# dt of a selective scan from ScalarE's softplus table, and silu of z where z is made

## Chip, cores and metric

The kernel runs on one core of a Trainium2 chip. The metric is the device time of one execution, in microseconds. All runs told here were in the fast state. "Before" is the tuned kernel, "after" the changed one. Engine names are those of the profile: PE (TensorE, products), DVE (VectorE), ACT (ScalarE), POOL (GpSimd). The granted clock is the share of the full TensorE clock that the profile shows, averaged over a stretch (PEclk).

## The reference, cut to what matters

Four images of 48 x 48 positions go through a layer with a two-dimensional selective scan, then attention, then a long spectral convolution.

```python
dts = einsum('bkrl,kdr->bkdl', dts_r, dt_proj_w)
dt  = softplus(dts + dt_proj_b)                      # what the change is about
...
def step(h, inp):                                    # scan over 2304 positions, 4 directions
    dA = exp(dt_l[..., None] * A)
    h  = h * dA + (dt_l * u_l)[..., None] * B_l
    y  = einsum('bkdn,bkn->bkd', h, C_l)
...
y = layernorm(y) * silu(z)                           # the change's second part
```

## The kernel before: the parts concerned

An image is scanned in 24 chunks of 384 positions (4 directions x 6), a chunk in 8 units (2 channel halves x 4 groups of states), a unit in 4 scans. Every engine works its instructions in the order of the program. Under the scans of images 1 to 3, PE runs the long convolution of the image before, fed in between so that it ends with the scans.

dt is prepared in pieces that are strewn over the units of the two chunks before. Softplus is built from relu, abs, exp and ln, all in one table set, and PE adds its four terms in PSUM:

```python
nc.scalar.activation(re[:, h, 1], ps[:, :CS], AF.Abs)       # per half, from PSUM
nc.scalar.activation(re[:, h, 0], ps[:, :CS], AF.Relu)
...
nc.scalar.activation(e, e, AF.Exp, scale=-1.0)              # both halves, 768 columns
nc.scalar.activation(u, e, AF.Identity, bias=1.0)
nc.scalar.activation(l, u, AF.Ln)
nc.scalar.activation(u, u, AF.Identity, bias=mone)
...
for h in range(NH):
    ps = mm_tile(...)                                       # one PSUM buffer of its own
    for i, (w, t) in enumerate(((ident, e[:, h]), (nident, u[:, h]), (ident, l[:, h]), (ident, re[:, h, 0]))):
        nc.tensor.matmul(ps[:, :CS], w, t, start=(i == 0), stop=(i == 3))
    nc.scalar.copy(re[:, h, 0], ps[:, :CS])                 # dt
    nc.vector.tensor_tensor(re[:, h, 1], ps[:, :CS], x, ALU.mult)   # dt * x, one operand in PSUM
```

The unit, which decides how waits spread:

```python
dA = exp(A * dt)                  # ACT, into one of two PSUM buffers, 4 per unit
tensor_tensor_scan(s, dA, s)      # DVE, 4 per unit
s = s * C                         # POOL, one product of 3.45 us per unit
y += csum^T s                     # PE
s_next = dt*x * B                 # DVE from PSUM (5 units of 8) or POOL (3 of 8)
```

Of the kernel before, what the change touches and what calls it, by code (L numbers as in the profile page):

```python
# [8 lines left out]
F32 = mybir.dt.float32  # L9
AF = mybir.ActivationFunctionType  # L10
ALU = mybir.AluOpType
# [4 lines left out]
P = 128  # L16
# [3 lines left out]
D, NS, R, K = 256, 16, 8, 4  # L20
NH = D // P
CS = 384
SUB = 384
# [31 lines left out]
def hybrid_kernel(ctx: ExitStack, tc: tile.TileContext, a: dict, out: bass.AP):  # L55
# [3 lines left out]
    nc = tc.nc  # L59
    ctx.enter_context(tc.manual_schedule())  # L60
    wp = ctx.enter_context(tc.tile_pool(name="w", bufs=1, side="left"))
# [5 lines left out]
    ident = wp.tile([P, P], F32, name="ident")  # L67
# [4 lines left out]
    def load(name, shape, src):  # L72
        t = wp.tile(shape, F32, name=name)
        nc.scalar.dma_start(t, src)
        return t

    win = load("win", [P, 2 * D], a["in_proj_wT"])
# [10 lines left out]
    owb = wp.tile([P, NH, C], F32, name="owb")  # L88
    nc.vector.tensor_scalar_mul(cw, cw, 0.5)
    nc.vector.tensor_scalar_mul(cb, cb, 0.5)  # L90
    for h in range(NH):
        nc.vector.tensor_scalar_mul(owb[:, h], owg[:, h], nb[:, h:h + 1])
        nc.vector.tensor_scalar_mul(owg[:, h], owg[:, h], ng[:, h:h + 1])
# [18 lines left out]
    nident = wp.tile([P, P], F32, name="nident")  # L112
# [11 lines left out]

    csum = wp.tile([P, DL], F32, name="csum")
    nc.vector.tensor_reduce(csum, ident.rearrange("p (c j) -> p j c", j=DL), AX.X, ALU.add)
    mone = wp.tile([P, 1], F32, name="mone")
    nc.vector.memset(mone, -1.0)
    shift = wp.tile([P, 1], F32, name="shift")
    nc.vector.memset(shift, -SHIFT)  # L130
    carry = wp.tile([P, NH, Q4, G4], F32, name="carry")
# [9 lines left out]
    def tokens(x, J):  # L141

        n = PIECES[J]
        return x[512 * J:512 * J + P * n].rearrange("(p j) c -> p j c", j=n)

    def exp_ln():

        nc.scalar.preload_act_table_set("natural_log_exp_and_others")

    def normed(x, d, eps, small, sq, name):  # L150

# [17 lines left out]
    def prologue(b, pool, mm_tile):  # L169
# [11 lines left out]
        xc = xcs[b] = [keep.tile([P, H, W], F32, tag=f"xc{h}", name=f"xc{b}_{h}") for h in range(NH)]  # L181
        rows, parts = SUB // W, SUB // P

        def cols(i):
            return slice(i * SUB, (i + 1) * SUB)
# [52 lines left out]
        def proj(h, i, z):  # L238
            now = {}

            def pe():
                now["ps"] = mm_tile(f"ip{b}_{h}_{i}_{z}")
                nc.tensor.matmul(now["ps"][:, :SUB], win[:, z * D + h * P:z * D + (h + 1) * P], xT[:, cols(i)],
                                 start=True, stop=True)

            def rest():
                if z:
                    t = pool.tile([P, SUB], F32, tag=f"z{i % 2}", name=f"z{b}_{h}_{i}")
                    nc.scalar.copy(t, now["ps"][:, :SUB])
                    nc.sync.dma_start(zs[h, :, cols(i)], t)  # L250
                    return
                nc.scalar.copy(xpad[:, 1 + i * rows:1 + (i + 1) * rows, 1:W + 1],
                               now["ps"][:, :SUB].rearrange("p (r w) -> p r w", w=W))
            tasks.append((pe, rest, not (h or i or z)))
# [27 lines left out]
        n = L // SUB  # L282
# [34 lines left out]
    def in_order(t, k, lo, n):  # L317

        if k % 2 == 0:
            return t[:, lo // W:(lo + n) // W, :]  # L320
        return t.rearrange("p h w -> p w h")[:, lo // H:(lo + n) // H, :]

    def mm_tile(name):
        return psm.tile([P, 512], F32, tag="mm", name=name)

    class Chunk:
# [16 lines left out]
        def prep(self, pool):  # L343




            k, name, xc = self.k, self.name, xcs[self.b]
            yield
            xd = self.xd = pool.xd.tile([64, CS], F32, tag="xd", name=f"xd{name}")  # L350
            bcd = self.bcd = dram.tile([32, CS], F32, tag="bcd", name=f"bcd{name}")
            ps = mm_tile(f"xp{name}")
            for h in range(NH):
                nc.tensor.matmul(ps[:64, :CS], xw[:, h, k, :], in_order(xc[h], k, self.lo, CS),
                                 start=(h == 0), stop=(h == NH - 1))
            yield 2 * CS
            nc.scalar.activation(xd, ps[:64, :CS], AF.Identity, bias=onerow)
            yield

            u, l = [pool.one.tile([P, NH, CS], F32, tag=f"tmp{v}", name=f"{v}{name}") for v in "ul"]  # L360
            re = pool.one.tile([P, NH, 2, CS], F32, tag="re", name=f"re{name}")
            for h in range(NH):
                ps = mm_tile(f"dt{name}_{h}")
                nc.tensor.matmul(ps[:, :CS], dtw[:, k, h * P:(h + 1) * P], xd[:R + 1], start=True, stop=True)
                yield CS
                nc.scalar.activation(re[:, h, 1], ps[:, :CS], AF.Abs)
                nc.scalar.activation(re[:, h, 0], ps[:, :CS], AF.Relu)
                if h == 0:
                    nc.sync.dma_start(bcd, xd[32:64])
                yield  # L370
            e = re[:, :, 1]
            yield 0
            nc.scalar.activation(e, e, AF.Exp, scale=-1.0)
            nc.scalar.activation(u, e, AF.Identity, bias=1.0)
            yield
            yield 0
            nc.scalar.activation(l, u, AF.Ln)
            nc.scalar.activation(u, u, AF.Identity, bias=mone)
            d = dram.tile([NH, DL, 2, G4, CS], F32, tag="dtdu", name=f"dtdud{name}")

            def store(h):
                for g in range(G4):
                    nc.sync.dma_start(d[h, :, :, g], re[g * DL:(g + 1) * DL, h])

            def load(h):
                rep = pool.rep.tile([P, 2, G4, CS], F32, tag="rep", name=f"rep{name}_{h}")
                for c in range(C4):
                    nc.sync.dma_start(rep[c * DL:(c + 1) * DL], d[h])
                self.rep.append(rep)

            yield
            for h in range(NH):
                ps = mm_tile(f"sp{name}_{h}")
                for i, (w, t) in enumerate(((ident, e[:, h]), (nident, u[:, h]), (ident, l[:, h]), (ident, re[:, h, 0]))):
                    nc.tensor.matmul(ps[:, :CS], w, t, start=(i == 0), stop=(i == 3))
                yield 4 * CS

                nc.scalar.copy(re[:, h, 0], ps[:, :CS])
                x = in_order(xc[h], k, self.lo, CS)
                w = x.shape[2]  # L400
                nc.vector.tensor_tensor(re[:, h, 1].rearrange("p (r w) -> p r w", w=w),
                                        ps[:, :CS].rearrange("p (r w) -> p r w", w=w), x, ALU.mult)
                if h == 1:
                    store(0)
                yield
            yield 0
            store(1)
            load(0)
            yield
            yield 0  # L410
            load(1)
            yield
# [60 lines left out]
    POOLED = ((0, 3), (1, 1), (1, 3))  # L473
    order = [(k, c) for k in range(K) for c in (range(NCH) if k < 2 else reversed(range(NCH)))]
    quads = [(h, q) for h in range(NH) for q in range(Q4)]
# [1 line left out]
    EARLY = 4  # L477
    FETCHED = sorted({q for h, q in POOLED} | set(range(Q4, 2 * Q4)))

    CHUNK_COLS = (len(quads) - len(POOLED)) * CS + len(quads) * CS + 12 * CS  # L480

    def begin_scans(b, pool):

# [12 lines left out]
    def scans(b, chunks, preps, front, sp, back, work, work_cols):  # L496

        units = [Unit(ch, h, q) for ch in chunks for h, q in quads]
        total = len(chunks) * CHUNK_COLS + work_cols
        done = [0]  # L500
# [75 lines left out]
    def epilogue(b, T, xn, xnT, tmp, pool, ps):  # L576
# [7 lines left out]
        zr, mu, o, sq, rd, lns, pt = {}, {}, {}, {}, {}, {}, {}  # L584
        var = ps.one.tile([P, 512], F32, tag="var", name=f"var{b}")

        def at(J):
            return slice(512 * J, 512 * J + P * PIECES[J])
# [7 lines left out]
        def means(J):  # L596
            n = P * PIECES[J]
            mu[J] = ps.two.tile([P, 512], F32, tag="mu", name=f"mu{b}_{J}")
            for h in range(NH):
                nc.tensor.matmul(mu[J][:, :n], dmean, yf[h][:, at(J)], start=(h == 0), stop=(h == NH - 1))  # L600
            nc.scalar.activation(zr[J][:, :, :n], zr[J][:, :, :n], AF.Silu)

        def center(J):
            n = P * PIECES[J]
# [460 lines left out]
        yield from stu(b, pool, ps)  # L1065
        pool.close()

    def exp_tanh():
        nc.scalar.preload_act_table_set("exp_and_others")

    turn = Stage(tc, "p", "left", one=(1, SB))
    begin0 = Stage(tc, "pp", "right", mm=(4, PSUM))
    once = Stage(tc, "once", "right", one=(1, SB))
    exp_tanh()
    run(prologue(0, turn.one, lambda name: begin0.mm.tile([P, 512], F32, tag="t", name=name)), 3, weights(once.one))
    exp_ln()
    turn.close()
    once.close()
    begin0.close()
# [3 lines left out]
    for b in range(B):  # L1083
        sp = Stage(tc, f"h{b}", "left", s=(6, SB))
        ps = Stage(tc, f"b{b}", "right", psa=(2, PSUM), psy=(1, PSUM), psB=(1, PSUM), psc=(2, PSUM), psp=(1, PSUM))
# [17 lines left out]
        ps = Stage(tc, f"e{b}", "right", one=(1, PSUM), two=(2, PSUM))  # L1103
# [14 lines left out]
                parts.pop(0)()  # L1118
        turn.close()
        if more:  # L1120
            exp_ln()
            front = Stage(tc, f"f{b + 1}", "left", one=(1, SB), xd=(2, SB), rep=(3, SB))
            pieces = begin_scans(b + 1, front)
        first = None
# [7 lines left out]
    ps = Stage(tc, "end", "right", psc=(4, PSUM), psp=(1, PSUM))  # L1132
# [52 lines left out]
```

## Time and profile before

| stage | us | fullest engine |
|---|---|---|
| opening | 127 | a chain |
| scan of image 0 ("first stage") | 1068 | DVE 89%, POOL 87% |
| scans of images 1, 2, 3 ("dense stages") | 1339, 1344, 1328 | PE 95%, DVE 80% |
| attention, three times between scans | 314 each | mixed |
| last attention and convolution | 993 | PE |

The prediction shows the stretches behind the table. The ACT groups that the change touches, from the view of groups on ACT: line, operation, operands and count, then busy us, mean ns, and idle time before with what ended it.

```profile
L366 ACT ACTIVATE re<-dt 128x384 f32<-128x384 f32 x192 | 93.4, 486 | 222.3 <-PE dt L364 202.2 <-DMA bc<-bcd 13.7 <-DMA dtdud<-re 2.3
...
L398 ACT COPY re<-sp 128x384 f32<-128x384 f32 x192 | 91.8, 478 | 440.7 <-PE sp L395 440.7
...
L374 ACT ACTIVATE u<-re 128x768 f32<-128x768 f32 x96 | 81.0, 844 | 3.3
L373 ACT ACTIVATE re<-re 128x768 f32<-128x768 f32 x96 | 79.5, 828 | 0.0
L377 ACT ACTIVATE l<-u 128x768 f32<-128x768 f32 x96 | 79.5, 828 | 0.0
```

Note the 440.7 us that ACT stands before its dt copies: it waits in its own order for PE to come to the four products. The dt x x product on DVE, from the view of that line (duration ns min/median/max):

```profile
L401 DVE TENSOR_TENSOR re<-sp,xc x192: 520/668/832, 104.7 to 6053.2; 128x384 f32<-128x384 f32 x192
```

### The profile page before, as it was taken

Reading aid. Unit: us, or ns where it says so; the run is one execution under the profiler, and the core shown is the slowest. Engines: PE = TensorE matmul, PEld = TensorE weight load, DVE = VectorE, ACT = ScalarE, POOL = GpSimd, SP = SyncE. Lnnn points to the kernel's source line nnn. Section 1 sums busy time; section 2 is a strip of 40 time slices with the busy share of each in tenths; the row PEclk is TensorE's granted clock in tenths of the full one; section 3 lists DMA queues with packets and bytes.
Section 4 is the critical chain, followed back from the end, with each engine's and each line's share of the span. In section 5 each row is a group of like instructions: output and inputs, shape, how many; then the busy total and the mean of one; then the engine's idle time right before and its main releaser. Section 6 shows DMA issues by size and latency. Waiting matters only on the chain. (4 is left out here: it accounts for less than half of the span.)

```text
span 7140.9 us, 79677 instructions
## 1 busy us (share of the span) xinstructions
PE 6335.6 (89%) x26760; PEld 3652.2 (51%) x26760; DVE 4863.0 (68%) x6145; ACT 2986.6 (42%) x5616; POOL 3849.3 (54%) x1815
## 2 busy tenths in 40 slices
PE   4777776888999998778999999788999999789999
PEld 2333333434555565534555556534555556547788
DVE  6898897557888876457888886447888887522111
ACT  3666664334445543334454543234454544231000
POOL 2888886036777765126677775205677776300000
PEclk7777777899999999899999999899999999899999
DMA  3555553046777765135767776125676777215545
GB/s 95 139 136 137 135 140 98 22 116 151 177 180 187 190 186 166 37 89 138 173 183 181 189 186 194 44 60 139 168 181 175 196 181 205 83 41 139 159 139 177
DMA packets 648922, 1019.14 MB, mean 143 GB/s; under 512 B 93849, under 2 KB 506649, under 8 KB 623778
## 3 DMA queue, kind: packets, MB, share of 16 engines
q1 hardware_dynamic: 642816, 1010.84, 54.3%
q8 instruction: 213, 3.49, 0.2%
q10 hardware_dynamic: 5698, 3.21, 0.2%
q14 instruction: 195, 1.60, 0.1%
HBM read 895.86 MB, written 117.84 MB: 142 GB/s over the span
## 5 line engine op out<-in xcount | busy, mean ns | idle before, releaser
L456 POOL TENSOR_TENSOR s<-s,bc 128x1536 f32<-128x1536 f32 x768 | 2645.1, 3445 | 260.5 <-DVE s L447 160.2
L447 DVE TENSOR_TENSOR_SCAN s<-dA,carry,s 128x384 f32<-128x384 f32 x2560 | 2440.0, 1001 | 253.5 <-ACT dA L444 251.8
L444 ACT ACTIVATE dA<-rep,A 128x384 f32<-128x384 f32 x3072 | 1753.1, 584 | 973.9 <-DVE s L447 956.2
L939 PE MATMUL cv<-tt,u 128*128 128x256 f32 (+4 forms) x7680 | 1686.6, 359 | 59.4 <-DVE U L959 39.8
L939 PEld LDWEIGHTS cv<-tt,u 128*128 128x128 f32 (+1 forms) x7680 | 1272.3, 191 | 670.2 <-issue 335.7
L959 DVE TENSOR_TENSOR U<-cv,Q 128x256 f32<-128x256 f32 (+1 forms) x1280 | 494.0, 392 | 1035.5 <-PE cv L939 1021.6
L439 POOL TENSOR_TENSOR s<-rep,bc 128x1536 f32<-128x1536 f32 x288 | 993.3, 3449 | 97.7 <-DMA bc<-bcd 97.7
L939 PE MATMUL cv<-tt,us 128*128 128x256 f32 (+4 forms) x3840 | 870.7, 363 | 78.9 <-DVE U L959 41.0
L439 DVE TENSOR_TENSOR s<-rep,B 128x1536 f32<-128x1536 f32 x480 | 834.5, 1739 | 100.6 <-PE B L431 84.6
L464 PE MATMUL y<-s,csum 128*32 128x384 f32 x6144 | 716.2, 541 | 169.1 <-POOL s L456 154.4
L939 PEld LDWEIGHTS cv<-tt,us 128*128 128x128 f32 (+1 forms) x3840 | 637.3, 192 | 321.5 <-issue 96.2
L948 ACT COPY Q<-cv 128x256 f32<-128x256 f32 (+3 forms) x640 | 224.0, 351 | 1377.9 <-PE cv L939 1242.3
L997 PE MATMUL pr<-U,G 128*128 128x512 f32 (+4 forms) x2048 | 717.6, 482 | 48.7 <-DMA G<-gd 40.5
L455 POOL COPY carry<-s 128x4 f32<-128x4 f32 x640 | 120.5, 188 | 1132.9 <-DVE s L447 1049.5
L431 PE MATMUL B<-xd,spread 32*128 32x384 f32 x960 | 475.0, 576 | 18.0 <-DVE s L439 18.0
L447 DVE TENSOR_TENSOR_SCAN s<-dA,s 128x384 f32<-128x384 f32 x512 | 457.1, 940 | 39.2 <-ACT dA L444 37.8
L997 PEld LDWEIGHTS pr<-U,G 128*128 128x128 f32 x2048 | 339.0, 194 | 251.6 <-issue 147.8
L464 PEld LDWEIGHTS y<-s,csum 128*32 128x32 f32 x6144 | 125.5, 111 | 603.4 <-issue 301.8
L700 PE MATMUL s<-xnT 128*128 128x512 f32 (+1 forms) x720 | 356.0, 580 | 51.8 <-ACT e L702 28.5
L702 ACT ACTIVATE e<-s,shift 128x512 f32<-128x512 f32 (+1 forms) x360 | 231.4, 644 | 335.2 <-PE s L700 335.0
L161 POOL TENSOR_TENSOR ln_vu<-ln_vu,mhalf 128x4 f32<-128x4 f32 (+1 forms) x20 | 31.4, 1571 | 623.1 <-DVE ln_vu L160 623.1
L693 PE MATMUL o<-e,xn 128*128 128x512 f32 (+1 forms) x720 | 340.2, 556 | 0.0
(167 smaller groups left out, 4883.4 us busy)
## 6 DMA issues: line engine op xcount, KB each, us to landing
rep<-dtdud SPq DMA_DIRECT2D x768, 384.0 KB, 7.8
tt<-fd SPq DMA_DIRECT2D x192, 577.0 KB, 4.2
bc<-bcd SPq DMA_DIRECT2D x2304, 48.0 KB, 3.7
tt<-fd SPq DMA_DIRECT2D x192, 513.0 KB, 4.2
tt<-fd SPq DMA_DIRECT2D x192, 385.0 KB, 3.8
dtdud<-re SPq DMA_DIRECT2D x768, 96.0 KB, 2.2
G<-gd SPq DMA_DIRECT2D x192, 256.0 KB, 4.8
tt<-fd SPq DMA_DIRECT2D x64, 514.0 KB, 5.4
```

Source lines behind the costliest of these rows:

```text
L431: nc.tensor.matmul(self.bt[:, :CS], spread[32:64, self.q].rearrange("p c j -> p (c j)"), self.ch.xd[32:64], start=True, stop=True)
L439: eng.tensor_tensor(s, self.ch.rep[self.h][:, 1], bt.unsqueeze(1).to_broadcast([P, G4, CS]), ALU.mult)
L444: nc.scalar.activation(dA[:, :CS], ch.rep[self.h][:, 0, g], AF.Exp, scale=A[:, ch.k, self.h * G4 + g, self.q:self.q + 1])
L447: nc.vector.tensor_tensor_scan(s, dA[:, CS - 1::-1] if ch.rev else dA[:, :CS], s, 0.0 if ch.first else carry[:, self.h, self.q, g:g + 1], ...
L456: nc.gpsimd.tensor_tensor(self.s, self.s, ch.bc[Q4 + self.q].unsqueeze(1).to_broadcast([P, G4, CS]), ALU.mult)
L464: nc.tensor.matmul(ch.y[g * DL:(g + 1) * DL, :CS], csum, self.s[:, g], start=(self.q == 0), stop=(self.q == Q4 - 1))
L693: nc.tensor.matmul(po[J][:, :w], xn[:, i], e[:, :w], start=(i == 0), stop=(i == NT - 1))
L700: nc.tensor.matmul(p[:, :w], xnT[:, i * P:(i + 1) * P], xnT[:, 512 * J:512 * J + w], start=True, stop=True)
L702: nc.scalar.activation(e[:, :w], p[:, :w], AF.Exp, bias=shift)
L939: nc.tensor.matmul(p2[:, :, at - first:], x, t[:kp, :, hi - 1 - at + J * P:end if end >= 0 else None:-1], start=(J == 0), stop=(J == nb - 1))
L959: nc.vector.tensor_tensor(dst, src, q, ALU.add)
L997: nc.tensor.matmul(p[:, :, :v], Gs[n][:, q, x, :], U[n][:, 4 * q:4 * q + 4, :v], start=False, stop=(k == KF - 1 and q == 1 and v == w))
```

## The change

Intent: take eight fp32 identity products per chunk off PE, which is the full engine of the dense stages, and most of the ACT chain with them, by using the table that holds softplus itself. The price is a switch to that table and back per chunk. Silu of z moves from the head of the attention stage to where z is projected, as tanh (same set as exp: the run exp_for_softplus below, which uses both, has one table load in the whole kernel) and one DVE operation.

```diff
-    nc.scalar.activation(re[:, h, 1], ps[:, :CS], AF.Abs)
-    nc.scalar.activation(re[:, h, 0], ps[:, :CS], AF.Relu)
+    nc.scalar.copy(re[:, h, 0], ps[:, :CS])
...
-e = re[:, :, 1]
+nc.scalar.activation(re[:, :, 0], re[:, :, 0], AF.Softplus)   # end of a chunk's unit 7
...  (Exp, Identity, Ln, Identity and the four products per half removed)
+def times_x(h):                                               # end of unit 0, middle of unit 1
+    nc.vector.tensor_tensor(dx, dt, x, ALU.mult)              # dt and x both in SBUF
...
-    nc.scalar.copy(t, now["ps"][:, :SUB])                     # z
+    nc.scalar.activation(t, now["ps"][:, :SUB], AF.Tanh)      # z weights halved
+    nc.vector.scalar_tensor_tensor(t, t, 1.0, now["ps"][:, :SUB], ALU.add, ALU.mult)
...
-    nc.scalar.activation(zr[J][:, :, :n], zr[J][:, :, :n], AF.Silu)
```

The requests to load the set with both exp and ln go too. And a counter changes: work that is fed in between the scans (the convolution; under image 0, which has none before it, the preparation of its filters) is paced by columns that PE has done, and a chunk now counts 12 - 8 = 4 times 384 columns for the preparation of dt (`CHUNK_COLS`). So fed-in work can fall into other units than before. The runs below change the counter along with the products: one_product has 6, products_back and products_late have 12.

More of the change, by code (lines that the diff above doesn't have):

```diff
@@ L90, in hybrid_kernel @@
     nc.vector.tensor_scalar_mul(cb, cb, 0.5)
+    nc.vector.tensor_scalar_mul(win[:, D:], win[:, D:], 0.5)
     for h in range(NH):
@@ L126, in hybrid_kernel @@
     nc.vector.tensor_reduce(csum, ident.rearrange("p (c j) -> p j c", j=DL), AX.X, ALU.add)
-    mone = wp.tile([P, 1], F32, name="mone")
-    nc.vector.memset(mone, -1.0)
     shift = wp.tile([P, 1], F32, name="shift")
@@ L144, in tokens @@
         return x[512 * J:512 * J + P * n].rearrange("(p j) c -> p j c", j=n)
-    def exp_ln():
-        nc.scalar.preload_act_table_set("natural_log_exp_and_others")
     def normed(x, d, eps, small, sq, name):
@@ L358, in prep @@
             yield
-            u, l = [pool.one.tile([P, NH, CS], F32, tag=f"tmp{v}", name=f"{v}{name}") for v in "ul"]
             re = pool.one.tile([P, NH, 2, CS], F32, tag="re", name=f"re{name}")
@@ L370, in prep @@
                 yield
-            e = re[:, :, 1]
+            nc.scalar.activation(re[:, :, 0], re[:, :, 0], AF.Softplus)
             yield 0
-            nc.scalar.activation(e, e, AF.Exp, scale=-1.0)
-            nc.scalar.activation(u, e, AF.Identity, bias=1.0)
-            yield
-            yield 0
-            nc.scalar.activation(l, u, AF.Ln)
-            nc.scalar.activation(u, u, AF.Identity, bias=mone)
             d = dram.tile([NH, DL, 2, G4, CS], F32, tag="dtdu", name=f"dtdud{name}")
@@ L389, in load @@
                 self.rep.append(rep)
+            def times_x(h):
+                x = in_order(xc[h], k, self.lo, CS)
+                dt, dx = [re[:, h, i].rearrange("p (r w) -> p r w", w=x.shape[2]) for i in range(2)]
+                nc.vector.tensor_tensor(dx, dt, x, ALU.mult)
             yield
-            for h in range(NH):
-                ps = mm_tile(f"sp{name}_{h}")
-                for i, (w, t) in enumerate(((ident, e[:, h]), (nident, u[:, h]), (ident, l[:, h]), (ident, re[:, h, 0]))):
-                    nc.tensor.matmul(ps[:, :CS], w, t, start=(i == 0), stop=(i == 3))
-                yield 4 * CS
-                nc.scalar.copy(re[:, h, 0], ps[:, :CS])
-                x = in_order(xc[h], k, self.lo, CS)
-                w = x.shape[2]
-                nc.vector.tensor_tensor(re[:, h, 1].rearrange("p (r w) -> p r w", w=w),
-                                        ps[:, :CS].rearrange("p (r w) -> p r w", w=w), x, ALU.mult)
-                if h == 1:
-                    store(0)
-                yield
+            times_x(0)
+            yield 0
+            times_x(1)
+            store(0)
+            yield
             yield 0
             store(1)
+            yield
+            yield 0
+            yield
+            yield 0
             load(0)
@@ L478, in hybrid_kernel @@
     FETCHED = sorted({q for h, q in POOLED} | set(range(Q4, 2 * Q4)))
-    CHUNK_COLS = (len(quads) - len(POOLED)) * CS + len(quads) * CS + 12 * CS
+    CHUNK_COLS = (len(quads) - len(POOLED)) * CS + len(quads) * CS + 4 * CS
     def begin_scans(b, pool):
@@ L1066, in stu_alone @@
         pool.close()
-    def exp_tanh():
-        nc.scalar.preload_act_table_set("exp_and_others")
     turn = Stage(tc, "p", "left", one=(1, SB))
@@ L1073, in hybrid_kernel @@
     once = Stage(tc, "once", "right", one=(1, SB))
-    exp_tanh()
     run(prologue(0, turn.one, lambda name: begin0.mm.tile([P, 512], F32, tag="t", name=name)), 3, weights(once.one))
-    exp_ln()
     turn.close()
@@ L1120, in hybrid_kernel @@
         if more:
-            exp_ln()
             front = Stage(tc, f"f{b + 1}", "left", one=(1, SB), xd=(2, SB), rep=(3, SB))
```

## The prediction

> **What bounds the kernel now.** I first cut the span where the scans start and stop and asked for the busy time of each engine in each stretch. Columns: the stretch and its length, then busy time and instruction count of PE, PEld, DVE, ACT, POOL, the granted TensorE clock, DMA share and GB/s.
>
> ```profile
> 0.00:127.00 127.00, 51.24 (x106) 23.18 (x106) 79.94 (x107) 33.69 (x63) 8.39 (x13) 0.72 0.34 84
> 127.00:1195.00 1068.00, 797.82 (x3068) 325.53 (x3068) 949.47 (x979) 642.72 (x1196) 924.94 (x423) 0.75 0.55 133
> 1195.00:1509.00 314.00, 247.76 (x738) 139.16 (x738) 136.99 (x220) 105.56 (x178) 36.06 (x30) 0.86 0.17 49
> 1509.00:2848.00 1339.00, 1268.71 (x5764) 728.37 (x5768) 1075.76 (x1304) 617.95 (x1177) 928.21 (x423) 0.98 0.68 174
> ...
> 6450.00:7141.00 691.00, 685.85 (x3292) 548.05 (x3292) 116.56 (x293) 52.53 (x148) 0.00 (x0) 1.00 0.51 155
> ```
>
> So there are three kinds of stage. The first scan stage (1068 us) is held by DVE (89%) with POOL right behind (87%); its PE has slack. The three later scan stages (1339, 1344 and 1328 us) run the previous image's long convolution under the scans, and PE is the full engine there: 1269 of 1339 us (95%), DVE 80%, ACT only 46%. The attention stages (about 314 us) and the last 691 us hardly touch the change. The three dense stages, 4011 us together, decide the result.
>
> Next, what the removed work costs PE there. The groups of PE instructions in the first dense stage (busy us, mean ns):
>
> ```profile
> L395 PE MATMUL sp<-re,ident 128*128 128x384 f32 x184 | 74.5, 486 | 0.0
> ...
> L395 PE MATMUL sp<-l,ident 128*128 128x384 f32 x92 | 37.2, 486 | 0.0
> L395 PE MATMUL sp<-u,nident 128*128 128x384 f32 x92 | 37.2, 486 | 0.0
> ```
>
> No idle time lies before them: they stand in a full queue. An fp32 product leaves two records that overlap, so I take the cost from starts in the timeline instead: groups of two products start at 2041.85, 2042.49, 2043.13 and 2043.78 us, that is 0.645 us per product of 384 columns. A chunk (24 to an image) has two halves of four products: 8 x 0.645 = 5.16 us.
>
> Third, cutting each dense stage at the first scan of each chunk (22 inner chunks): a chunk takes 55.2 us, PE is busy 53.1 and idle 2.2; DVE is busy 45.0 and idle 10.3, of which 5.3 wait for convolution results, 3.5 for ACT's exponentials and 0.9 for the dt copy. In the first scan stage a chunk takes 44.5 us, DVE busy 39.9, idle 4.7 (ACT exponentials 1.8, spread-B products 1.3, the y sum 0.85, the dt copy 0.7).
>
> **What the Trainium skill says.** "ScalarE: Activation LUTs", section "What ACT_TABLE_LOAD costs", puts a switch at about 1283 ns of load plus 1380 ns of drain. The trace agrees on the load and shows no such drain: ACT is back at work 0.01 us later.
>
> ```profile
> 1425.58 0.69 ACT L702 ACTIVATE e<-s,shift 128x512 f32<-128x512 f32 x1
> 1426.29 1.28 ACT L148 ACT_TABLE_LOAD   x1
> 1427.59 0.69 ACT L702 ACTIVATE e<-s,shift 128x512 f32<-128x512 f32 x1
> ```
>
> The same page, section "Table sets: the hidden batching unit", has exp and tanh in one set, the cheap functions (copy, identity) in every set, and lists no softplus; with the change's own words I take softplus to lie in a set without exp. Then each of the 96 chunks pays two loads, one before its softplus and one before the next exponential; no run here shows it yet.
>
> "SBUF — State Buffer", section "Who interferes with whom", says that a DVE instruction with two SBUF inputs contends with a GpSimd instruction that reads SBUF, and whoever starts second blocks until the first is done. This matters: before, every two-tensor DVE operation of the scan loop has one operand in PSUM (L401 multiplies PSUM sp by x). After, dt x x reads both from SBUF beside a POOL that is 70 to 87% busy. The trace shows the block where it occurs now: an operation of 693 ns median takes 3.90 us, ending half a microsecond after POOL's product.
>
> ```profile
> 1496.92 3.90 DVE L163 TENSOR_TENSOR u<-u,ln_vu 128x512 f32<-128x512 f32 x1 [1.18 <-POOL ln_vu L161]
> ...
> 1496.85 3.42 POOL L439 TENSOR_TENSOR s<-rep,bc 128x1536 f32<-128x1536 f32 x1
> ```
>
> "TensorE: Matmul & The Clock Gate", part 1, says that idle stretches throttle the array and activity releases it. The trace fits: clock 0.98 where PE is dense, 0.75 in the first scan stage.
>
> **The change part by part**, per chunk unless said.
>
> PE: minus 5.16 us, on the bound of the dense stages. PE side afterwards 55.2 - 5.2 = 50.0 us.
>
> ACT: removed are two Abs and two Relu (0.49 each), Exp 0.83, Identity 0.84, Ln 0.83, Identity 0.94: 5.4 us. The two copies stay. Added: Softplus on 768 columns, by Exp's duration 0.83, and two loads with their gaps, 2.6. ACT gets 2 us lighter, off the path. But the pieces lie differently. The softplus is issued at the end of a chunk's last unit, right before the next unit's exponentials, so ACT does load, softplus, load: 3.45 us in one piece. I took, at each chunk boundary, when ACT falls free, when the buffer of the next exponential falls free and when DVE began the next scan, and put 3.45 us in: the first scan would start 1.35 us later on average in the first scan stage and 1.6 us in the dense ones (3.6 us at eight or nine boundaries of 23, nothing at seven). In exchange the two bursts of 1.7 us in units 0 and 1 go; they carry 1.8 us of DVE's waits for ACT in the first scan stage and 0.8 in the dense ones. The waits for the dt copy (0.7 and 0.9) go too.
>
> DVE: the two products keep their size (677 ns now), but take the shared port. The first is issued after the last scan of unit 0, just when POOL starts its 3.45 us product on that unit or is still in one (left of it then: 1.0 us on average in the first stage). Where convolution additions come in between, POOL goes first and DVE stands for most of 3.45 us. The second falls in unit 1, where POOL is mostly idle for 2 us. I put 2.0 us per chunk on DVE in the dense stages and 1.3 in the first, estimates from these lengths.
>
> Silu at z: per image 12 more DVE products from PSUM, about 0.5 us each (estimate from the 384-column operations), 6 us where DVE has room (137 of 314 us); only in the opening 127 us do they lie on the path. Off go five Silu (1.04 us each) and two table loads at the head of each attention stage.
>
> Sum. First scan stage: minus 1.8 and 0.7, plus 1.35 and 1.3: nothing, 1068 us stays. Dense stages: PE 50.0; DVE 45.0 busy + 2.0 port + 1.6 burst + 2.0 left of the other waits for ACT = 50.6. Two engines equally full, in order, with two convolution buffers between them, don't overlap perfectly: I add 1.2 us, my choice, and get 51.8. Gain 3.4 x 24 x 3 = 245 us. Attention stages: one chunk's sp products (5.2 us of PE) and the silu chain, 7 us each for three and 3 for the last, 24 us. Opening: about 8 us less of products and copies in the first chunk's preparation, 6 more of DVE: nothing. Total 7160 - 245 - 24 = about 6890 us.
>
> **The rivals.** *PE alone decides*: all 5.16 us come back in each dense chunk, 72 x 5.16 = 372, with attention 6765 us. For it: PE's idle is only 2.2 us per chunk while DVE has 10.3. Against it: DVE needs 45 us plus waits. *DVE takes over*: port blocks hit both products (3 us each) and the burst shows whole; a dense chunk needs 45 + 6 + 3.4 + 2 = 56 us and the first stage loses 24 x 5 = 120 us: about 7280 us. Against it: POOL is idle at the second product, and part of the burst hides. *The clock falls*: DVE's new blocks open gaps in PE and the gate throttles, as in the first stage; a clock of 0.93 instead of 0.98 makes PE's 48 busy us into 50.4, and the time about 7030. Against it: PE keeps over 90% of the stage. *Table switches cost their stated 2.66 us*: 2.7 us more at each of 96 boundaries, partly hidden, perhaps 100 to 150 us: 7000 us. Against it: the trace above.
>
> **Range and chances.** The centre is 6890. Between the PE rival and half of the DVE rival lies 6790 to 7000, which I give 8 in 10. Two per cent is 143 us, a line at 7017: faster by over 2% 0.89, within 0.10, slower 0.01.
>
> **What would show it.** The dense stages at 1245 to 1265 us each with PE at about 92%, and the first at 1050 to 1090; no sp products; 192 table loads in the scans, each 1.28 us; the softplus at 0.83 us; the two-SBUF product with a mean well over 0.68 us and single ones at 3 us or more; first scans of a chunk waiting for ACT. Wrong would be: a product that never blocks (then towards 6800), a clock under 0.95 in the dense stages, or a first scan stage that moves by over 40 us.

## The result

After: 7054.03 us median (7047.04 to 7058.19, 4 runs); before in the same rounds 7157.26 us. The ratio is 0.9859 (95% interval 0.9842 to 0.9876). A ratio here is the mean time of one kernel's fast runs over that of the other's of the same rounds, so not quite the ratio of the medians. That is 103 us faster, under the 2% line, outside the predicted range and 164 us above its centre.

The stretches of the profile of after, cut in the same way:

```profile
0.00:124.00 124.00, 48.43 (x90) 20.03 (x90) 84.90 (x119) 25.69 (x45) 8.40 (x13) 0.67 0.35 86
124.00:1215.00 1091.00, 681.05 (x2700) 255.28 (x2700) 969.22 (x980) 608.41 (x1090) 935.07 (x423) 0.68 0.56 131
1215.00:1521.00 306.00, 246.56 (x722) 136.68 (x722) 142.11 (x232) 97.26 (x164) 35.98 (x30) 0.86 0.16 45
1521.00:2830.00 1309.00, 1185.56 (x5400) 672.03 (x5400) 1089.59 (x1305) 595.76 (x1063) 934.27 (x423) 0.95 0.73 179
...
6362.00:7051.00 689.00, 683.84 (x3286) 546.65 (x3284) 116.56 (x293) 52.40 (x147) 0.00 (x0) 1.00 0.52 155
```

PE went down as planned in the dense stage, by 83 us (1268.71 to 1185.56), but the stage became only 30 us shorter: PE now stands for 123 of 1309 us where it stood for 70 of 1339. All three dense stages together went from 4011 to 3927 us, minus 84, where I had said 245. The first stage went from 1068 to 1091, plus 23, where I had said nothing. The attention stages gave 8 us each, 24 together, as predicted; the opening 3.

The new work on ACT, in its groups:

```profile
L365 ACT ACT_TABLE_LOAD x95 | 121.9, 1283 | 1.7
L432 ACT ACT_TABLE_LOAD x89 | 114.2, 1283 | 4.5 <-DMA rep<-dtdud 3.0
L361 ACT COPY re<-dt 128x384 f32<-128x384 f32 x192 | 91.7, 477 | 179.7 <-PE dt L359 166.4 <-DMA dtdud<-re 6.4 <-DMA rep<-dtdud 2.1
L365 ACT ACTIVATE re<-re 128x768 f32<-128x768 f32 x96 | 81.0, 843 | 1.1
```

Softplus is as long as exp (843 ns), and both switches are there, 1283 ns each. In order of time, at one chunk's boundary, first ACT, then DVE (start, us, engine, line, operation; in brackets the idle time before and what ended it):

```profile
2151.74 0.58 ACT L432 ACTIVATE dA<-rep,A 128x384 f32<-128x384 f32 x1 [0.32 <-DVE s L435]
2152.34 1.28 ACT L365 ACT_TABLE_LOAD   x1
2153.63 0.84 ACT L365 ACTIVATE re<-re 128x768 f32<-128x768 f32 x1
2154.49 1.28 ACT L432 ACT_TABLE_LOAD   x1
2155.79 1.09 ACT L432 ACTIVATE dA<-rep,A 128x384 f32<-128x384 f32 x2
```

```profile
2151.62 1.90 DVE L435 TENSOR_TENSOR_SCAN s<-dA,carry,s 128x384 f32<-128x384 f32 x2
2153.49 0.42 DVE L946 TENSOR_TENSOR U<-cv,Q 128x256 f32<-128x256 f32 x1
2153.83 1.74 DVE L427 TENSOR_TENSOR s<-rep,B 128x1536 f32<-128x1536 f32 x1
2156.41 1.92 DVE L435 TENSOR_TENSOR_SCAN s<-dA,carry,s 128x384 f32<-128x384 f32 x2 [0.84 <-ACT dA L432]
```

Load, softplus, load take 3.45 us, and the next scan comes 0.84 us late: the rest was hidden by what DVE had in hand. And the dt x x product, whose line answers to the one of before, and one of its long ones beside POOL:

```profile
L382 DVE TENSOR_TENSOR re<-re,xc x192: 524/797/4065, 102.9 to 5958.6; 128x384 f32<-128x384 f32 x192
```

```profile
2162.46 2.28 DVE L382 TENSOR_TENSOR re<-re,xc 128x384 f32<-128x384 f32 x1
```

```profile
2160.89 3.44 POOL L444 TENSOR_TENSOR s<-s,bc 128x1536 f32<-128x1536 f32 x1 [0.19 <-DVE s L435]
```

The POOL product ends at 2164.33; the DVE product, which starts at 2162.46, ends 0.41 us later. In the dense stages the first of a chunk's two products takes 1.64 us on average (0.69 before), the second 0.68: 0.95 us per chunk. POOL pays a little too: its carry copies went from 188 to 228 ns on average.

Who waits for whom in a dense stage, before and then after (sum in us, times, longest us):

```profile
DVE U L959 <- PE cv L939: 139.8, 164, 5.3
DVE s L447 <- ACT dA L444: 85.0, 75, 3.5
PEld cv L939 <- DVE U L959: 56.4, 67, 2.4
PE cv L939 <- DVE U L959: 28.1, 29, 2.0
```

```profile
PEld cv L926 <- DVE U L946: 122.5, 86, 7.4
DVE s L435 <- ACT dA L432: 110.9, 72, 6.2
DVE U L946 <- PE cv L926: 98.6, 115, 6.5
PE cv L926 <- DVE U L946: 82.5, 52, 7.0
```

DVE waits less for PE, but still 98.6 us; PE waits three times as long for DVE to take convolution results out of PSUM, up to 7 us at once. Each now waits for the other.

### The profile page after: what moved, and what is told of

Read it like the earlier page. It is cut to its first block, busy times and chain, and to the rows that moved or that the text cites. A ratio compares the mean times of both kernels' runs of the same rounds, so it can differ in the third digit from the quotient of the medians.

```text
span 7051.1 us, 75955 instructions
## 1 busy us (share of the span) xinstructions
PE 5958.7 (85%) x25224; PEld 3407.3 (48%) x25224; DVE 4944.7 (70%) x6193; ACT 2846.0 (40%) x5101; POOL 3877.9 (55%) x1815
## 4 chain that ended last, share of the span: by engine, by line
PE 48%; DVE 24%; DMA 12%; ACT 6%; POOL 4%; issue 4%; SPq 2%; ACTq 0%; DVEq 0%; POOLq 0%
PE cv L926 22%; DVE s L435 12%; PE pr L984 6%; DMA rep<-dtdud 4%; DVE s L427 4%; PE y L452 4%; PE s L687 3%; PE o L680 3%; DMA bc<-bcd 3%; POOL s L444 3%; PE B L419 3%; DVE re L382 2%; DMA tt<-fd 2%; PE xp L350 2%; PE op L623 2%
## 5 line engine op out<-in xcount | busy, mean ns | idle before, releaser
L926 PEld LDWEIGHTS cv<-tt,u 128*128 128x128 f32 (+1 forms) x7680 | 1288.1, 193 | 720.9 <-issue 303.7
L926 PE MATMUL cv<-tt,us 128*128 128x256 f32 (+4 forms) x3840 | 897.6, 371 | 149.0 <-DVE U L946 111.2
L452 PE MATMUL y<-s,csum 128*32 128x384 f32 x6144 | 749.3, 563 | 210.9 <-POOL s L444 122.8
L926 PEld LDWEIGHTS cv<-tt,us 128*128 128x128 f32 (+1 forms) x3840 | 652.3, 197 | 429.7 <-DVE U L946 160.1
L984 PE MATMUL pr<-U,G 128*128 128x512 f32 (+4 forms) x2048 | 753.1, 500 | 68.2 <-DVE U L946 36.5
L443 POOL COPY carry<-s 128x4 f32<-128x4 f32 x640 | 145.9, 228 | 1005.4 <-DVE s L435 872.5
L419 PE MATMUL B<-xd,spread 32*128 32x384 f32 x960 | 494.7, 598 | 73.4 <-DVE s L427 72.7
L799 PE MATMUL G<-M,W 128*128 128x128 f32 (+2 forms) x768 | 232.0, 452 | 162.5 <-DMA M<-in_M_phi_plus 109.5
```

Of the source, the lines that this page charges most:

```text
L419: nc.tensor.matmul(self.bt[:, :CS], spread[32:64, self.q].rearrange("p c j -> p (c j)"), self.ch.xd[32:64], start=True, stop=True)
L452: nc.tensor.matmul(ch.y[g * DL:(g + 1) * DL, :CS], csum, self.s[:, g], start=(self.q == 0), stop=(self.q == Q4 - 1))
L799: nc.tensor.matmul(p[:, :n] if j else p[:, NF - 1 - i], W[:, q if t else 0, i], M[t][:, i].unsqueeze(1).to_broadcast([P, n, C]) if j else ...
L926: nc.tensor.matmul(p2[:, :, at - first:], x, t[:kp, :, hi - 1 - at + J * P:end if end >= 0 else None:-1], start=(J == 0), stop=(J == nb - 1))
L984: nc.tensor.matmul(p[:, :, :v], Gs[n][:, q, x, :], U[n][:, 4 * q:4 * q + 4, :v], start=False, stop=(k == KF - 1 and q == 1 and v == w))
```

## The experiments

The theories after the result. A: the table switches and the piece of 3.45 us ate the gain. B: DVE and PE are too unevenly loaded from unit to unit, so freed PE time turns into mutual waits whatever else is done. C: the port that the two-SBUF product shares with GpSimd ate it. Stage lengths below are from the first to the last scan of an image in the profiled run; "chunk" is the mean of 22 inner chunks, cut at each chunk's first scan, averaged over the dense stages. Waits count idle stretches of over 0.1 us. "Dense" is the sum of the three stages. The median is that of all runs, the other columns come from the one profiled run, which can lie off it: before 15 us below its median, softplus_port 20 below, loads_twice and products_late 19 above. Over 72 dense chunks 20 us are 0.3 us a chunk, so smaller differences between chunks are not read.

| kernel | median us | first stage | dense | dense chunk | PE busy | PE waits for DVE | DVE busy | DVE waits for ACT |
|---|---|---|---|---|---|---|---|---|
| before | 7157 | 1068 | 4011 | 55.2 | 53.0 | 1.3 | 45.0 | 4.4 |
| after | 7054 | 1091 | 3927 | 54.1 | 49.2 | 4.2 | 45.5 | 4.7 |
| exp_for_softplus | 6967 | 1093 | 3835 | 52.7 | 48.7 | 3.6 | 45.6 | 3.3 |
| one_product | 6863 | 1028 | 3782 | 51.8 | 49.3 | 1.7 | 44.6 | 2.9 |
| exp_ln_set | 6980 | 1091 | 3852 | 53.0 | 49.0 | 3.5 | 45.5 | 3.5 |
| exp_ln_psum | 6871 | 1044 | 3795 | 52.2 | 48.6 | 3.0 | 44.5 | 3.7 |
| softplus_port | 6987 | 1072 | 3857 | 53.1 | 48.8 | 3.6 | 44.5 | 4.8 |
| loads_twice | 7163 | 1106 | 4032 | 55.4 | 49.9 | 4.8 | 45.5 | 6.2 |
| silu_at_z | 7157 | 1071 | 4019 | 55.3 | 53.1 | 1.3 | 45.0 | 4.4 |
| exp_ln_pool | 6833 | 1092 | 3705 | 50.8 | 48.2 | 2.1 | 43.3 | 3.4 |
| products_back | 7578 | 1160 | 4344 | 59.7 | 54.5 | 4.5 | 45.0 | 8.7 |
| exp_ln_mixed | 6790 | 1043 | 3716 | 51.0 | 48.4 | 2.0 | 43.3 | 3.4 |
| softplus_mid | 7174 | 1138 | 3998 | 55.2 | 49.8 | 4.9 | 45.8 | 5.2 |
| products_late | 7117 | 1022 | 4065 | 56.2 | 53.3 | 2.3 | 44.8 | 4.1 |

**exp_for_softplus**

```diff
-nc.scalar.activation(re[:, :, 0], re[:, :, 0], AF.Softplus)
+nc.scalar.activation(re[:, :, 0], re[:, :, 0], AF.Exp)
```

> The changed kernel with Exp in place of Softplus (values wrong on purpose): everything stays but the 192 table loads, since exp is in the set that is loaded anyway. Theory A (the load-softplus-load piece of 3.45 us ahead of a chunk's first exponentials is what ate the gain, with its knock-on in units 7, 0 and 1): 6850 to 6920 us, dense stages about 1255 us each, first scan stage about 1055. Theory B (DVE and PE are simply too unevenly loaded from unit to unit, so freed PE time turns into waits of each for the other whatever ACT does): 7000 to 7040 us. Theory C (the port that the two-SBUF product shares with GpSimd): also 7000 to 7040, since the product stays.

6967.35 us (6958.16 to 6974.68), ratio to before 0.9731 (0.9714 to 0.9749). The comparison with the reference passed it, although exp isn't softplus: that comparison can't tell the two apart on these inputs, and the kernel is no candidate. One load is left in the whole kernel, where after has 191. The loads are worth 87 us, all of it in the dense stages; the first stage didn't move at all. Between A and B: more than B allows, less than A asks.

**one_product**

```diff
-for i, (w, t) in enumerate(((ident, e[:, h]), (nident, u[:, h]), (ident, l[:, h]), (ident, re[:, h, 0]))):
-    nc.tensor.matmul(ps[:, :CS], w, t, start=(i == 0), stop=(i == 3))
+nc.tensor.matmul(ps[:, :CS], ident, re[:, h, 0], start=True, stop=True)
```

> The kernel before with one identity product per half instead of four (values wrong on purpose), so 3.87 us of PE work per chunk go and nothing else: ACT chain, waits, PSUM operand of the dt x x product all stay. Theory A or C (PE's work comes back once loads and port are out of the way): about three quarters of it in the 72 dense chunks, 6930 to 6990 us. Theory B: 7080 to 7130 us, dense stages over 1310 us.

6862.51 us (6853.35 to 6870.25), ratio 0.9589; values wrong as intended (relative error 0.089). This is more than any theory gave: three quarters of the products off, with their columns out of the counter, bring 297 us. The dense chunk falls by 3.4 us for 3.87 us of work, so B falls in its pure form: PE time does come back. Even the first stage, where PE has slack, gains 40 us.

**exp_ln_set**

```diff
-nc.scalar.copy(re[:, h, 0], ps[:, :CS])
+nc.scalar.activation(re[:, h, 0], ps[:, :CS], AF.Exp)
-nc.scalar.activation(re[:, :, 0], re[:, :, 0], AF.Softplus)
+nc.scalar.activation(re[:, :, 0], re[:, :, 0], AF.Ln, bias=1.0)
 # and the set with exp and ln requested before each image's scans, as before
```

> The changed kernel with dt = Ln(Exp(.) + 1) from the one set that has both (values right): Exp read from PSUM in place of the copy, Ln with bias 1 in place of Softplus, no table load in the scans. Product still from two SBUF operands. Theory A: as exp_for_softplus within 20 us, 6850 to 6920. Theories B and C: 7000 to 7040.

6979.65 us (6972.67 to 6982.9), ratio 0.9748, values right (by a comparison that exp alone passed too, so this says little; the formula is softplus). With softplus as Ln(Exp + 1) there are no switches in the scans and the gain is near that of exp_for_softplus (75 us instead of 87). In the first stage again nothing, and its product line shows why: the first product of a chunk takes 2.65 us there on average, against 1.45 us in after. When ACT no longer holds DVE up, DVE meets POOL at the port instead.

**exp_ln_psum**

```diff
+ps = mm_tile(...)
+nc.scalar.activation(ps[:, :CS], re[:, h, 0], AF.Ln, bias=1.0)   # per half, into PSUM
+nc.scalar.copy(re[:, h, 0], ps[:, :CS])
-nc.vector.tensor_tensor(dx, re[:, h, 0], x, ALU.mult)
+nc.vector.tensor_tensor(dx, ps[:, :CS], x, ALU.mult)
```

> As exp_ln_set, but Ln goes half by half into PSUM, a copy takes dt to SBUF, and DVE multiplies from PSUM, so that no DVE operation of the scan loop has two SBUF inputs (values right; ACT 1.1 us more per chunk). Theory C, from the 1.0 us by which the first product of a chunk was longer than before: 60 to 100 us faster than exp_ln_set. Theory A alone: within 25 us of exp_ln_set, either way. Theory B: within 25 us, both near 7020.

6871.01 us (6854.31 to 6875.45), ratio 0.9593, values right. C's number: 109 us under exp_ln_set, though ACT has more to do; 47 of them in the first stage. The product of exp_ln_set and then of exp_ln_psum:

```profile
L386 DVE TENSOR_TENSOR re<-re,xc x192: 525/828/3848, 102.1 to 5878.9; 128x384 f32<-128x384 f32 x192
```

```profile
L388 DVE TENSOR_TENSOR re<-ln,xc x192: 519/662/837, 102.0 to 5777.1; 128x384 f32<-128x384 f32 x192
```

With one operand in PSUM none is longer than 0.84 us.

**softplus_port**

```diff
+ps = mm_tile(...)
+nc.scalar.copy(ps[:, :CS], re[:, h, 0])       # softplus and its loads stay
-nc.vector.tensor_tensor(dx, re[:, h, 0], x, ALU.mult)
+nc.vector.tensor_tensor(dx, ps[:, :CS], x, ALU.mult)
```

> The changed kernel, with its Softplus and its two loads per chunk, but ACT copies dt to PSUM and DVE multiplies from there (values right; ACT 1 us more per chunk): only the shared port goes. If the costs add (each wait that is put on DVE lengthens the stage, as exp_ln_set to exp_ln_psum gained 108 us): 6930 to 6970 us, first scan stage 1045 to 1060 us. If one hides behind the other (with the loads in place DVE's port waits fall into time that it waits for ACT anyway): over 7000 us.

6987.13 us (6966.73 to 6997.99), ratio 0.9766: in between. With the loads in place the port is worth 67 us, without them 109. The four corners are 7054 (both), 6980 (port alone), 6987 (loads alone) and 6871 (neither): together the two cost 183 us, singly 109 and 116. They overlap in part but by no means hide each other.

**loads_twice**

```diff
 store(0)
 yield
+nc.scalar.activation(dummy, shift, AF.Softplus)      # one column, end of unit 1
 yield 0
```

> The changed kernel with one more Softplus, of a single column, per chunk at the end of unit 1 (values right): two more table loads, 2.8 us of ACT per chunk, at another place. If a load costs about what exp_for_softplus gave back (87 us for the pair, 1.3 us per dense chunk): 7110 to 7180 us. If the place matters and DVE has enough in hand at the end of unit 1: within 30 us of the changed kernel, about 7060 us. If the loads of exp_for_softplus were worth only what came from their position at the chunk's boundary, the dense stages do not move.

7163.03 us (7143.72 to 7182.51, 20 runs), ratio 1.0009: a second pair costs 109 us, 1.3 us per dense chunk, as the first pair gave back. All of the change's gain is gone.

```profile
L434 ACT ACT_TABLE_LOAD x181 | 232.2, 1283 | 6.0 <-DMA rep<-dtdud 2.8
```

This line of its ACT groups, the loads before an exponential, has about twice the count of after (89).

**softplus_mid**

```diff
 nc.scalar.copy(re[:, h, 0], ps[:, :CS])
+if h == 1: nc.scalar.activation(re[:, :, 0], re[:, :, 0], AF.Softplus)   # middle of unit 7
 yield
-nc.scalar.activation(re[:, :, 0], re[:, :, 0], AF.Softplus)              # end of unit 7
```

> The changed kernel with its Softplus half a unit earlier, in the middle of unit 7 between the second and the third exponential (values right). If the place of the 3.45 us piece decides (fewer DVE operations in hand there, two scans and no 1.7 us product): 7080 to 7130 us. If a pair of loads costs the same wherever it stands (loads_twice: 109 us at the end of unit 1): 7040 to 7070.

7173.71 us (7163.03 to 7187.84), ratio 1.0016: 120 us more than after, beyond even the upper branch. The place matters, for nothing else was moved. The reason put forward, that DVE has less in hand between the second and third exponential than at the end of the unit, covers only part of it. In the dense chunks DVE's wait for ACT moves from unit 0 (1.8 to 0.1 us) to unit 7 (0.3 to 2.3 us), which is 0.35 us more of 1.1. In the first stage, which grows by 47 us, about half is the port: a chunk's first product there takes 2.4 us on average, against 1.5 in after. The changed kernel had already put its softplus at the better of these two places.

**silu_at_z** (the change's second part alone, on the kernel before; the diff is that of the change, the exp and ln set kept)

> The kernel before with only the silu of z moved to where z is made. By the stages of the two traces (attention 306 instead of 314 us, three times, the last and the opening by 1 to 3 us): 20 to 30 us faster than before, about 7130 us, with all four scan stages as before to 5 us. If those 8 us per attention stage came from the shorter dt preparation instead: less than 10 us.

7157.45 us (7144.3 to 7172.85), ratio 0.9997 (0.9988 to 1.0005): nothing. The attention stages stay at 314 to 317 us. So the 8 us per attention stage of after do not come from the silu of z; by exclusion they come from the shorter preparation of the next image's first chunk there. Two other traces agree: exp_ln_set, which asks for the exp and ln set again, keeps its attention stages at 306 to 308 us, and one_product, with the old silu, has 308 to 311.

**exp_ln_pool**

```diff
-nc.vector.tensor_tensor(dx, dt, x, ALU.mult)
+nc.gpsimd.tensor_tensor(dx, dt, x, ALU.mult)         # on exp_ln_set
```

> exp_ln_set with the dt x x product on GpSimd instead of DVE (values right): no two-SBUF operation on DVE, DVE 1.4 us lighter per chunk, POOL about 1.8 us heavier. If DVE's load is what counts: 6800 to 6870 us, dense stages about 1245. If POOL, at 87% of the first stage, becomes the bound there: first scan stage 1075 to 1100 and the whole at 6890 to 6940.

6833.04 us (6829.23 to 6852.45), ratio 0.9551. Both branches came true, each in its stage: the dense stages fall to 1230 to 1245 us, DVE being 1.2 us lighter than in exp_ln_psum (the chunk follows by 1.4 us), and the first stage stays at 1092, with POOL at 40.8 of 45.9 us per chunk.

**exp_ln_mixed** (the product on POOL for images 1 to 3, on DVE from PSUM for image 0)

> The product on GpSimd in the three dense stages, where POOL has room, and on DVE from PSUM in the first, where it has none (values right, no table load in the scans). Sum of the stages measured: first as exp_ln_psum 1044, dense as exp_ln_pool 1230 to 1245, rest unchanged: 6775 to 6800 us. If the stages influence each other: up to 6840.

6789.98 us (6773.65 to 6802.23), ratio 0.9476 (0.9457 to 0.9495), values right. The stages add up as expected. It beats both kernels: 5.2% under before.

**products_back** (exp_ln_psum, plus four unread products per half through the PSUM buffer that Ln uses next)

> exp_ln_psum with eight identity products per chunk that nobody reads (values right): PE gets back exactly the 5.16 us per chunk that the change took from it, paced as before; nothing else moves. If PE's work lies on the path of the dense stages in full: 72 x 5.16 = 372 us more than exp_ln_psum, 7240 us. If the difference between before and exp_ln_psum is all PE work: 7150 to 7170. If part of that gain came from ACT's shorter chain and the dt copy's wait: 7050 to 7120, dense stages about 1320.

7578.34 us, ratio 1.0574: a miss, and a badly made test. The buffer is a single one, so ACT's Ln waited for products at the end of PE's queue, and DVE for ACT:

```profile
ACT ln L387 <- PE waste L385: 826.2, 192, 20.0
```

**products_late** (the same products at the ends of units 2 and 3, where nobody waits for the buffer)

> products_back put ACT behind PE's queue (its Ln had to wait for the one PSUM buffer), so it did not measure PE's work alone. Here the same eight unread products per chunk stand at the ends of units 2 and 3, behind the last use of that buffer for a chunk and with nothing waiting for them (values right). If PE's time is the path of the dense stages in full: 72 x 5.16 = 372 us more than exp_ln_psum, about 7240, dense chunks 57.3 us. If the freed PE time was worth what one_product gave back (3.4 us of dense chunk for 3.87 us of work): 300 to 330 more, about 7190, dense chunks 56.6. If most of the old cost was the wait of ACT for these products: under 7080. First scan stage within 25 us of 1044 either way, since PE has slack there.

7117.48 us (7116.27 to 7136.08), ratio 0.9955: 246 us more than exp_ln_psum, between the branches. The dense stages get 270 us longer, 4.1 us per chunk for 5.16 us of PE work; the first stage is 22 us shorter, its granted clock 0.78 instead of 0.68 and DVE's waits for ACT 0.3 us per chunk instead of 1.8. The dense chunk, 56.2 us, is also 1.0 us longer than before's, which has the same products and a longer ACT chain besides. So the products' cost depends on where they stand, and 4.1 us is not what they cost in every place.

## Why the prediction was wrong

**The bound was right.** PE is the path of the dense stages for most of its work: products_late pays 4.1 of 5.16 us, one_product gets 3.4 of 3.87 us back. Without the two side costs the removal is worth 289 us (before to exp_ln_psum, the shorter ACT chain included), 217 of them in the dense stages.

**The two sums of the dense chunk were near, too.** The DVE sum was 50.6. Measured: busy 45.5, which contains 0.95 for the port, and 4.7 of waits for ACT, together 50.2. The port was half of what I had put, since only about half of a chunk's first products were blocked in the dense stages, the waits for ACT 1.1 us more. PE was to be 50.0 with its idle; measured 49.2 busy, 1.4 us above before's 53.0 less 5.16, while the granted clock fell from 0.98 to 0.95.

**The step that failed is the allowance**: "Two engines equally full, in order, with two convolution buffers between them, don't overlap perfectly: I add 1.2 us, my choice, and get 51.8." The measured chunk is 54.1, so the term is 3.9 us against the larger sum. On DVE's side it stands for the waits for convolution results that are left: 5.3 us per chunk before, put at 1.2, measured 3.8. The sum took for granted that DVE's new stalls would take the place of these waits, as if idle time were a reserve. The runs show that it isn't one: taking the loads away gives 0.9 to 1.4 us per dense chunk, taking the port away 0.8 to 1.0, and both 1.9.

Per unit the trace of after shows where it happens. DVE waits for ACT 1.8 us in unit 0 (about 0.45 before). PE then waits 2.3 us in units 0 and 1 to have convolution results taken (0.3 before), while in units 2, 4 and 6 DVE still waits 2.6 us for PE. Time lost in one unit isn't made up in another. That the two buffers are the reason is argued, not shown: no run changed their number, or the places of the fed-in work alone. The table tells it in one column: PE's waits for DVE per dense chunk are 1.3 us before, 4.2 after, 3.6 without loads or without port, 3.0 without both, and 2.1 when DVE loses the product as well.

Of the 5.16 us per dense chunk taken from PE, 1.1 came back where 3.4 were forecast. The two side costs took 1.9 (133 us in all), which is shown. Another 2.2 are lost even without them (exp_ln_psum: 52.2 us), already more than the 1.8 that the prediction had put down for everything. This part stays open between uneven units, as theory B has it, and the clock: seen from PE, after misses the predicted 51.8 us by 1.4 us of busy time at a lower clock and 0.9 us of idle.

**The first stage** was to stay and lost 23 us. I had let 2.5 us of gains and 2.65 us of costs cancel per chunk. The wait in unit 0 is as put (1.23 us for 1.35) and the port below (0.84 for 1.3), but DVE waits for ACT 2.9 us per chunk where 1.35 were to be left: 1.65 us of new waits for exponentials stand in units 2, 4 and 5. The misread line is the gain: "they carry 1.8 us of DVE's waits for ACT in the first scan stage", said of the two bursts in units 0 and 1. In the trace of before nearly all of these waits (1.78 of 1.81 us) stand behind other ACT work, with or without a burst in front of it: the copy `Gm`, and mostly a block of it and eight copies `W`, 2.8 us in all, which prepare the convolution's filters. One such wait before, first ACT, then DVE:

```profile
716.37 0.94 ACT L378 ACTIVATE u<-u,mone 128x768 f32<-128x768 f32 x1
717.22 0.46 ACT L817 COPY Gm<-G 128x384 f32<-128x384 f32 x1
...
719.63 0.39 ACT L800 ACTIVATE W<-nident,ws 128x128 f32<-128x128 f32 x1
719.92 1.07 ACT L444 ACTIVATE dA<-rep,A 128x384 f32<-128x384 f32 x2
```

```profile
720.52 1.93 DVE L447 TENSOR_TENSOR_SCAN s<-dA,carry,s 128x384 f32<-128x384 f32 x2 [2.08 <-ACT dA L444]
```

In after the burst is gone, the block is not. It now stands before late exponentials in units 2 and 4, and the wait is as long in unit 4 and 1.3 to 1.6 us in unit 2:

```profile
513.09 0.47 ACT L804 COPY Gm<-G 128x384 f32<-128x384 f32 x1
...
515.51 0.39 ACT L787 ACTIVATE W<-nident,ws 128x128 f32<-128x128 f32 x1
515.80 1.07 ACT L432 ACTIVATE dA<-rep,A 128x384 f32<-128x384 f32 x2
```

```profile
516.40 1.93 DVE L435 TENSOR_TENSOR_SCAN s<-dA,carry,s 128x384 f32<-128x384 f32 x2 [2.05 <-ACT dA L432]
```

These waits make 1.2 of the 1.65 us; the rest, in unit 5, stands behind ACT's read of the x projection, for which it waits on PE. That the block moved because the counter changed is likely and not shown alone. products_late, with the old count, has 0.3 us of such waits in all, but the products are back there too. That port and loads stand in for each other here is shown: no gain without loads alone, 47 us when the port goes as well.

**Attention and opening**: 24 us as predicted, but my reason was half wrong, since the silu of z alone brings nothing.

**The rivals.** "PE alone decides" was 6765; the nearest to it, exp_ln_mixed, needs no loads, no port and a lighter DVE and reaches 6790. "DVE takes over" had both side costs, but only 3 or 4 of 23 second products in a stage were blocked; and its own figures (56 us per dense chunk and 120 us in the first stage) add up to over 7310, not 7280. "The clock falls", at 7030 the rival nearest to the measured 7054, came in part: a clock of 0.95 where I had feared 0.93, and 49.2 busy us of PE where it had 50.4. The runs don't separate whether the lower clock made gaps or came of them. Switches of 2.66 us didn't occur. Of 192 loads forecast in the scans 176 fell there, since those for an image's first two chunks lie before its scans.

## What to carry to other kernels

When two engines hand work to each other in order, do not count idle time of the second one as a reserve. Here, with 10.3 us of it per chunk, stalls still lengthened the stage by most of their size, so count them in full unless the trace shows work in hand that covers them. When the removed work also paced other work, look where that other work lands: here a block of ACT copies kept its price in another place. Before moving an operand from PSUM to SBUF, look whether GpSimd is busy: here the products with two SBUF operands cost nearly as much as the table switches of 96 chunks (109 and 116 us, each alone). And before reaching for a special table, see whether two passes from a loaded set do the same; Ln(Exp + 1) did, and with the product fed from PSUM it was faster than the change by 183 us.

## What the Trainium skill lacked or had wrong

- "ScalarE: Activation LUTs", section "What ACT_TABLE_LOAD costs": it counts about 1380 ns of drain per switch beside the load. All loads here took 1283 ns, nearly all with 0.01 to 0.02 us of gap on each side; no drain shows.
- The same page's list of table sets names no set for softplus. Here softplus needed a load each way beside exp (190 loads in all scans and attention stages), while copies and identities between needed none. Softplus took 843 ns for 768 columns, like exp at 828.
- "SBUF — State Buffer", section "Who interferes with whom": confirmed (a product of 0.66 us took up to 4.07 us; all 70 long ones in after began while a POOL product ran and ended 0.4 to 0.7 us after it). What it lacks is a sense of size in a mixed kernel: 67 to 109 us of some 7000 for 192 products, of which about a third were blocked (70 in after and 83 in exp_ln_set took over 0.85 us, none before).
- No page tells how much of a stall on a less busy engine reaches the end when two engines are coupled by two buffers: here 1.9 us per chunk came back for the 0.95 us of port and the pair of loads.
